# Dispatch transfers of the last layer: one per four experts in place of one per expert, and one more step in the routing

## The chip, the cores and the metric

The kernel runs on one core of a Trainium2 chip. The metric is device time in microseconds (us) of one execution of the whole program, the median over runs. The core has five engines with a queue of instructions each: TensorE (PE, with its weight loads as PEld), VectorE (DVE), ScalarE (ACT), GpSimd (POOL) and SyncE (SP, which here only issues DMAs). An engine runs its own queue in order and waits on semaphores for the others.

## The reference

Four layers follow each other on x of 16 x 256 tokens with 128 features, all in float32; each is `x = x + s(LN(x)) * silu(g(LN(x)))`, with an attention-like part s and a feed-forward part g. The change touches the end of layer 2, whose g is a mixture of 32 experts that is computed for every token and every expert:

```python
sel = jax.nn.sigmoid(x2 @ sel_w)
scores, idx = jax.lax.top_k(sel, K)                                  # K = 4 of 32
gate = (jax.nn.one_hot(idx, E, dtype=sel.dtype) * scores[..., None]).sum(-2)
h = jax.nn.relu(jnp.einsum('bsd,edh->bseh', x2, keys))
moe_out = jnp.einsum('bseh,ehd,bse->bsd', h, values, gate)
```

and layer 3, whose s is a Mamba block in both directions (a scan over time, 256 channels, 16 states) and whose g routes every token to 2 of 16 experts with a limited capacity:

```python
vals, idx = jax.lax.top_k(probs, K)                                  # K = 2 of 16
oh_e = jax.nn.one_hot(idx_flat, E, dtype=x.dtype)
pos = (jnp.cumsum(oh_e, axis=0) * oh_e).sum(axis=1) - 1              # place in the expert's queue
within = (pos < C).astype(x.dtype)                                   # C = 640
expert_inputs = jnp.zeros((E, C, d), x.dtype).at[idx_flat, pos_c].add(x_pair)
expert_outputs = jax.vmap(_mlp)(expert_inputs, w_gate, w_up, w_down)
```

## The kernel before

The 4096 tokens lie in 32 tiles of 128 partitions. Layer 2's experts run in `ffn2`: for each of 8 chunks t of 512 tokens and each of 32 experts e there is one *unit*. PE multiplies by `keys` (L1081, into `f_ph`), ACT takes the relu (L1083, into `f_h`), PE multiplies by `values` (L1112, into `f_po`, two buffers), and DVE adds the product, times the gate, to `f_acc` (L1117, four instructions). A chunk ends with a silu on ACT (L1091) and two DVE operations (L1093, L1095), which give the new x of the chunk.

Between the units a hand-written order advances generators, one step (up to the next `yield`) per unit from e = 4 on: at t = 4 the routing of layer 3 for tiles 0 to 15 (`route.tiles(0, 16, mamba)`), at t = 5 the first work item of Mamba (`mamba.begin()`), at t = 7 the routing of tiles 16 to 27. What a generator has left when the next one begins is run through at once, ahead of expert 4 of that chunk; this happens with the first one at t = 5. The queues of PE, DVE, ACT and POOL hold instructions in just the order in which the program writes them.

`route.tiles` is `norms` (the layer norm of layer 3) and then `places`: logits, softmax, the two best of 16 (L1590 to L1593), a 0/1 mask (L1598 on DVE), the sums of the mask over the tokens ahead and over the tile (two matmuls on PE at L1604), running counts (L1613 to L1619), the place of each token in its expert's queue (L1622 to L1629), and the weights and the int32 index `f_at` (L1632 to L1636). Then four entries per tile go on the list `todo`: two choices j, each with a row of x (i = 0) and its weight and number (i = 1).

`route.scatter` takes one entry off that list and has POOL issue an indirect transfer that writes the 128 rows of a tile to their places in DRAM (`f_xd`, 512 bytes a row, or `f_md`, 8 bytes a row), through `put_rows` (L1358). With `apart` set, as in layer 2, it first puts a memset of one element (L1644) in POOL's queue:

```python
def scatter(self, apart=False):
    if self.todo:
        if apart:
            self.net.nc.gpsimd.memset(self.dot, 0.0)
        i, k, j = self.todo.pop(0)
        rows = self.meta[:, j, k, :] if i else self.net.xn[:, k, :]
        self.net.put_rows((self.xd, self.md)[i], self.at[:, j, k : k + 1], rows, self.sent[i])
```

Before the change layer 2 calls it once per unit with e >= 4. Nothing in POOL's queue waits for the experts: POOL runs a transfer as soon as the instruction before it is done, its index is written, and the transfer eight before it has landed.

What is left on the list goes out in `Mamba3.run`: 16 work items (8 pairs of sequences, two directions), each of 16 units (8 pairs of states times 2 halves of the channels), one transfer after every second unit (L1962), so 128 places in all. A unit of this stage: POOL forms the products (L1827), ACT the factors (L1842), DVE the scans (L1853) and a product with C (L1953), PE spreads C (L1863) and sums over the states (L1957). The products are made two pairs of states ahead. In each work item the first half of the next one (`first`) is run between the units: it stores `m_rows` (L1760) and has POOL do L1782, L1785, L1788 and L1792. The last item also takes the routing of tiles 28 to 31, whose 16 transfers go out at its end; `layer3` issues what is left on the list, and `ffn3` loads `f_md` and `f_xd` for the experts of layer 3.

Of the kernel before, what the change touches and what calls it, by code (L numbers as in the profile page):

```python
# [23 lines left out]
def bc(ap, n):  # L24

    return ap.unsqueeze(len(ap.shape)).to_broadcast([*ap.shape, n])


def bc1(ap, n):

    return ap.unsqueeze(1).to_broadcast([ap.shape[0], n, *ap.shape[1:]])


class Net:
# [988 lines left out]
    def ffn2(self, c, w, left, last):  # L1023
# [35 lines left out]
        route = Route3(self, last)  # L1059
# [12 lines left out]
        with ExitStack() as ctx:  # L1072
            sb = ctx.enter_context(tc.tile_pool(name="l2m", bufs=2))
            ps = ctx.enter_context(tc.tile_pool(name="l2m_ps", bufs=2, space=PSUM))
            long = {4: route.tiles(0, 16, mamba), 5: mamba.begin(), 7: route.tiles(16, 12, mamba)}
            short = now = iter(())
            units = [(t, e) for t in range(NCH) for e in range(NE)]

            def hidden(t, e):
                ph = ps.tile([P, 512], F32, name="f2_ph")  # L1080
                nc.tensor.matmul(ph, lhsT=keys[:, e, :], rhs=self.xnT[:, t * 512 : (t + 1) * 512], start=True, stop=True)  # L1081
                hT = sb.tile([P, 512], F32, name="f2_h", bufs=3)
                nc.scalar.activation(hT, ph, AF.Relu)  # L1083
                return hT

            def gated(t):

                k4 = slice(4 * t, 4 * t + 4)
                yield
                g = sb.tile([P, 4, D], F32, name="gate_t")  # L1090
                nc.scalar.activation(g, acc[:, k4, :], AF.Silu)  # L1091
                yield
                nc.vector.tensor_tensor(g, g, self.s[:, k4, :], ALU.mult)  # L1093
                yield
                nc.vector.tensor_tensor(self.x[:, k4, :], self.x[:, k4, :], g, ALU.add)  # L1095

            ahead = hidden(0, 0)
            for u, (t, e) in enumerate(units):
                if e == 4 and t in long:
                    for _ in now:  # L1100
                        pass
                    now = long[t]
                next(short, None)
                if e >= 4:
                    next(now, None)
                    route.scatter(True)
                hT = ahead
                if u + 1 < len(units):
                    ahead = hidden(*units[u + 1])
                po = ps.tile([P, 4, D], F32, name="f2_po")  # L1110
                for k in range(4):
                    nc.tensor.matmul(  # L1112
                        po[:, k, :], lhsT=hT[:, k * P : (k + 1) * P], rhs=values[:, e, :], start=True, stop=True
                    )
                for k in range(4):
                    n = 4 * t + k
                    nc.vector.scalar_tensor_tensor(  # L1117
                        acc[:, n, :], po[:, k, :], gate[:, n, e : e + 1], acc[:, n, :], ALU.mult, ALU.add
                    )
                if e == NE - 1:  # L1120
                    short = gated(t)
            for f in (short, now):
                for _ in f:
                    pass
# [334 lines left out]
class Route3:  # L1459
# [98 lines left out]
    def places(self, k0, n, mamba):  # L1558
        net, nc, NE = self.net, self.net.nc, self.NE
        kn = slice(k0, k0 + n)  # L1560
        (_, _, c), part = self.parts(n, mamba)
        pr, rep, l = part(0, 0, 24), part(0, 384, 24), part(0, 768, NE)
        mask, pos, fits, over = (part(1, 256 * i, NE) for i in range(4))
        wt, hit, m8 = part(2, 0, NE), part(2, 256, NE), part(2, 784, 8)
        run = c[:, 512 : 512 + 16 * (n + 1)].rearrange("p (n w) -> p n w", w=NE)
        den = c[:, 912 : 912 + n]
        ab = c[:, 928 : 928 + 2 * n].rearrange("p (j n) -> p j n", j=2)
        mx = c[:, 992 : 992 + n]
        pl = mamba.bank()[:, : n * NE].rearrange("p (n w) -> p n w", w=NE)
        for k in range(n):  # L1570
            o = (k0 + k) * P
            nc.tensor.matmul(pl[:, k, :], lhsT=net.xnT[:, o : o + P], rhs=self.rw, start=True, stop=True)
        nc.gpsimd.memset(pr[:, :, NE:], -1.0)
        self.count(hit, [[0, n], [int(self.CAP), NE]], 1, 0)
        self.count(over, [[P * NE, n], [1, NE]], self.rows + 1 + k0 * P * NE, NE)
        yield
        nc.vector.tensor_tensor(l, pl, bc1(self.rb, n), ALU.add)
        nc.vector.tensor_reduce(mx, l, AX.X, ALU.max)
        nc.vector.tensor_tensor(l, l, bc(mx, NE), ALU.subtract)
        yield  # L1580
        nc.scalar.activation(l, l, AF.Exp)
        yield
        nc.vector.tensor_reduce(mx, l, AX.X, ALU.add)
        nc.vector.reciprocal(mx, mx)
        nc.vector.tensor_tensor(pr[:, :, 0:NE], l, bc(mx, NE), ALU.mult)
        yield

        for g in range(0, n, 4):
            for k in range(g, g + 4):
                nc.vector.max(out=m8[:, k, :], in_=pr[:, k, :])  # L1590
            nc.vector.memset(m8[:, g : g + 4, 2:8], -1.0)
            for k in range(g, g + 4):
                nc.vector.match_replace(  # L1593
                    out=rep[:, k, :], in_to_replace=m8[:, k, :], in_values=pr[:, k, :], imm_value=-2.0
                )
            if g + 4 < n:
                yield
        nc.vector.tensor_tensor(mask, pr[:, :, 0:NE], rep[:, :, 0:NE], ALU.not_equal)  # L1598
        yield

        t = mamba.bank()
        pin, tot = (t[:, 256 * j : 256 * j + n * NE].rearrange("p (n w) -> p n w", w=NE) for j in range(2))
        for q, m in ((pin, self.tri), (tot, net.ones)):
            nc.tensor.matmul(q, lhsT=m, rhs=mask, start=True, stop=True)  # L1604
        yield

        nc.vector.tensor_tensor(den, m8[:, :, 0], m8[:, :, 1], ALU.add)
        nc.vector.tensor_scalar_add(den, den, 1e-9)
        nc.vector.reciprocal(den, den)
        nc.vector.tensor_tensor(wt, mask, bc(den, NE), ALU.mult)  # L1610
        nc.vector.tensor_tensor(wt, wt, pr[:, :, 0:NE], ALU.mult)
        yield
        nc.vector.tensor_copy(run[:, 0, :], self.before)  # L1613
        for k in range(n):
            nc.vector.tensor_tensor(run[:, k + 1, :], run[:, k, :], tot[:, k, :], ALU.add)
        nc.vector.tensor_copy(self.before, run[:, n, :])
        nc.vector.tensor_tensor(pos, pin, run[:, 0:n, :], ALU.add)
        nc.vector.tensor_single_scalar(fits, pos, self.CAP, ALU.is_lt)
        nc.vector.tensor_tensor(wt, wt, fits, ALU.mult)  # L1619
        yield  # L1620

        nc.vector.tensor_tensor(pos, pos, hit, ALU.add)  # L1622
        nc.vector.tensor_tensor(pos, pos, over, ALU.subtract)
        nc.vector.tensor_tensor(pos, pos, fits, ALU.mult)
        nc.vector.tensor_tensor(pos, pos, over, ALU.add)
        nc.vector.tensor_tensor(pos, pos, mask, ALU.mult)
        nc.vector.tensor_reduce(ab[:, 0, :], pos, AX.X, ALU.max)
        nc.vector.tensor_reduce(ab[:, 1, :], pos, AX.X, ALU.add)
        nc.vector.tensor_tensor(ab[:, 1, :], ab[:, 1, :], ab[:, 0, :], ALU.subtract)  # L1629
        yield  # L1630
        for j in range(2):
            nc.vector.tensor_tensor(hit, pos, bc(ab[:, j, :], NE), ALU.is_equal)  # L1632
            nc.vector.tensor_tensor(hit, hit, wt, ALU.mult)
            nc.vector.tensor_reduce(self.meta[:, j, kn, 1], hit, AX.X, ALU.add)
        nc.vector.tensor_scalar_add(ab, ab, -1.0)
        nc.vector.tensor_copy(self.at[:, :, kn], ab)  # L1636
        self.todo += [(i, k, j) for k in range(k0, k0 + n) for j in range(2) for i in range(2)]
        yield
# [414 lines left out]
```

## Time and profile before

| | us |
|---|---|
| median of 3 runs | 4148.38 |
| lowest and highest run | 4143.59, 4153.01 |
| the profiled execution | 4153.89 |
| its span, first to last instruction | 4152.2 |
| busy in that span: PE, DVE, ACT, POOL | 3626.3, 2987.9, 2126.9, 1918.5 |
| mean granted clock of TensorE | 0.95 |

The parts that matter here, by the timeline of the same execution: the units of layer 2's experts run up to about 2922, Mamba from there to 3933, the experts of layer 3 to 4152. An instruction's row gives its start, its length, its engine and line, and, in brackets, how long the engine sat idle before it and what ended that wait. Consecutive instructions of one kind are merged into a row (x8). The end of a matmul is modelled. "Granted clock" is the share of its full clock that TensorE got in a stretch. In the chain of waits, "another core or an unknown queue" is a wait whose end the profile can put down to no engine of this core.

### The profile page before, as it was taken

The numbers are of one execution on the slowest core, as the hardware profiler recorded it, in microseconds if no ns is written. First come the engines' busy times: TensorE is split into PE (matmuls) and PEld (weight loads), VectorE is DVE, ScalarE is ACT, GpSimd is POOL, SyncE is SP. The second block draws the span as 40 slices with busy tenths as digits, with TensorE's granted clock in tenths as the row PEclk, the third lists the DMA queues.
The fourth block names the chain that finished last, engine by engine and source line by source line (L and its number), as shares of the span: only waits on it lengthen the run. The fifth ranks groups of instructions, "written<-read, shape, count | busy, mean of one in ns | idle before, by whom it ended". The sixth has DMA issues, their size and how long they took to land. (4 is left out here: it accounts for less than half of the span.)

```text
span 4152.2 us, 61413 instructions
## 1 busy us (share of the span) xinstructions
PE 3626.3 (87%) x21623; PEld 2323.1 (56%) x21623; DVE 2987.9 (72%) x6273; ACT 2126.9 (51%) x4623; POOL 1918.5 (46%) x1979
## 2 busy tenths in 40 slices
PE   5689999875999999999999999769788899899795
PEld 3467777543566666777777776546333333333353
DVE  5467767575888887666666667636888999999834
ACT  2356666642777775444545333223565665666322
POOL 5974444000444443433333100250789877777634
PEclk8899999986999999999999899979899999999998
DMA  8365554320000001000000300010111211121123
GB/s 301 126 212 182 195 194 175 42 78 6 1 1 1 1 1 42 1 1 1 1 1 1 115 1 1 7 35 1 65 66 66 84 64 66 75 82 62 52 81 100
DMA packets 87366, 268.90 MB, mean 65 GB/s; under 512 B 18176, under 2 KB 34088, under 8 KB 81555
## 3 DMA queue, kind: packets, MB, share of 16 engines
q1 hardware_dynamic: 80403, 255.46, 18.0%
q0 software_dynamic: 6656, 9.52, 0.7%
q8 instruction: 172, 2.82, 0.3%
q14 instruction: 135, 1.11, 0.1%
HBM read 192.96 MB, written 71.97 MB: 64 GB/s over the span
## 5 line engine op out<-in xcount | busy, mean ns | idle before, releaser
L1827 POOL TENSOR_TENSOR m_h<-m_B,m_dtu 128x1024 f32<-128x1024 f32 x256 | 597.5, 2358 | 108.2 <-PE m_y L1957 104.1
L1853 DVE TENSOR_TENSOR_SCAN m_h<-m_a,m_h 128x512 f32<-128x512 f32 x512 | 601.3, 1208 | 40.1 <-ACT m_a L1842 34.8
L1957 PE MATMUL m_y<-m_h,ident 128*128 128x512 f32 x1024 | 513.8, 631 | 24.0 <-DVE m_h L1953 23.5
L883 POOL TENSOR_TENSOR a_e<-a_e,a_sm 128x512 f32<-128x512 f32 x256 | 263.8, 1041 | 445.2 <-DVE a_sm L882 351.5
L1117 DVE SCALAR_TENSOR_TENSOR f_acc<-f_po,f_gate,f_acc 128x128 f32<-128x128 f32 x1024 | 287.6, 344 | 219.8 <-PE f_po L1112 152.3
L1112 PEld LDWEIGHTS f_po<-values_sb,f_h 128*128 128x128 f32 x2048 | 277.5, 198 | 207.9 <-issue 130.5
L1957 PEld LDWEIGHTS m_y<-m_h,ident 128*128 128x128 f32 x1024 | 184.1, 195 | 340.3 <-issue 246.1
L398 DVE TENSOR_TENSOR a_e<-a_s,a_c 128x384 f32<-128x384 f32 x256 | 216.3, 845 | 189.9 <-PE a_s L395 183.6
L1189 POOL TENSOR_TENSOR r_g<-r_t 128x256 f32<-128x256 f32 x256 | 183.5, 728 | 360.3 <-DVE r_t L1188 357.2
L1083 ACT ACTIVATE f_h<-f_ph 128x512 f32<-128x512 f32 x256 | 152.2, 596 | 384.4 <-PE f_ph L1081 310.9
L1112 PE MATMUL f_po<-values_sb,f_h 128*128 128x128 f32 x2048 | 282.3, 283 | 71.5 <-ACT f_h L1083 46.6
L1220 ACT ACTIVATE r_e<-r_s,r_mx 128x256 f32<-128x256 f32 x512 | 208.0, 474 | 260.9 <-DVE r_mx L1214 260.8
L1953 DVE TENSOR_TENSOR m_h<-m_h,m_C 128x1024 f32<-128x1024 f32 x256 | 307.1, 1200 | 26.0 <-PE m_C L1863 26.0
L1188 DVE TENSOR_TENSOR r_t<-r_pp,trig_sb 128x512 f32<-128x512 f32 x256 | 169.5, 683 | 207.5 <-PE r_pp L1179 206.3
L876 ACT ACTIVATE a_e<-a_e,a_mx 128x256 f32<-128x256 f32 x512 | 255.1, 500 | 54.6 <-DVE a_sm L882 48.2
L1081 PE MATMUL f_ph<-xnT_sb,keys_sb 128*128 128x512 f32 x512 | 273.6, 618 | 0.4 <-ACT f_gate L1048 0.4
L403 ACT ACTIVATE a_e<-a_e,a_mx 128x128 f32<-128x128 f32 (+1 forms) x512 | 218.6, 453 | 93.0 <-DVE a_mx L399 65.0
L1208 PE MATMUL r_s<-pe_sb,r_g 128*128 128x256 f32 x1024 | 260.7, 388 | 0.0
L373 POOL COPY a_st<-a_p 128x192 f32<-128x192 f32 x256 | 135.7, 532 | 243.5 <-PE a_s L394 160.9
L1842 ACT ACTIVATE m_a<-m_dt,bA_sb 128x510 f32<-128x510 f32 x256 | 170.9, 686 | 141.3 <-DVE m_h L1853 140.4
L1863 PE MATMUL m_C<-m_dbc,ident 32*128 32x512 f32 x512 | 149.1, 655 | 96.6 <-DVE m_h L1953 92.3
L1842 ACT ACTIVATE m_a<-m_dt,fA_sb 128x510 f32<-128x510 f32 x256 | 169.9, 685 | 101.3 <-DVE m_h L1853 100.4
(476 smaller groups left out, 8227.5 us busy)
## 6 DMA issues: line engine op xcount, KB each, us to landing
m_B<-m_rows SPq DMA_DIRECT2D x32, 2048.0 KB
a_p<-pc SPq DMA_DIRECT2D x32, 768.0 KB
a_c<-cs SPq DMA_DIRECT2D x32, 768.0 KB
cs<-a_es SPq DMA_DIRECT2D x64, 256.0 KB
pc<-a_es SPq DMA_DIRECT2D x64, 256.0 KB
a_p<-pc SPq DMA_DIRECT2D x32, 512.0 KB
a_c<-cs SPq DMA_DIRECT2D x32, 512.0 KB
cs<-bg SPq DMA_DIRECT2D x8, 768.0 KB
```

The costliest lines, as they stand in the source:

```text
L403: nc.scalar.activation(e[:, cols], e[:, cols], AF.Exp, bias=mx[:, i : i + 1])
L876: nc.scalar.activation(e[:, i, :], e[:, i, :], AF.Exp, bias=mx[:, i : i + 1], accum_out=sm[:, i : i + 1])
L883: nc.gpsimd.tensor_tensor(e, e, bc(sm, S), ALU.mult)
L1081: nc.tensor.matmul(ph, lhsT=keys[:, e, :], rhs=self.xnT[:, t * 512 : (t + 1) * 512], start=True, stop=True)
L1112: nc.tensor.matmul(po[:, k, :], lhsT=hT[:, k * P : (k + 1) * P], rhs=values[:, e, :], start=True, stop=True)
L1117: nc.vector.scalar_tensor_tensor(acc[:, n, :], po[:, k, :], gate[:, n, e : e + 1], acc[:, n, :], ALU.mult, ALU.add)
L1208: nc.tensor.matmul(s[h][:, i, :], lhsT=G[:, i * P : (i + 1) * P], rhs=w["pe"], start=False, stop=i == 1)
L1827: nc.gpsimd.tensor_tensor(h, st["B"][n // 8][:, m : m + 2, :], bc1(st["dtu"][:, k, :], 2), ALU.mult)
L1842: nc.scalar.activation(f[:, :, 1:], sts[d]["dt"][:, k, :].rearrange("p (b t) -> p b t", b=2)[:, :, 1:], AF.Exp, scale=w[work[d][1]]["A"][: ...
L1853: nc.vector.tensor_tensor_scan(h[:, j, :], ready.pop(0), h[:, j, :], 0.0, op0=ALU.mult, op1=ALU.add)
L1953: nc.vector.tensor_tensor(h, h, sts[d]["C"], ALU.mult)
L1957: nc.tensor.matmul(sts[d]["y"][k], lhsT=net.ident, rhs=h[:, j, :], start=False, stop=n + j == N - 1)
```

## The change

Two edits. In `ffn2` the transfer is issued only at every fourth expert (e = 4, 8, ..., 28) in place of at each one from 4 on. In `places` a `yield` is put between the mask and the two matmuls that sum it, so that these come one step later in all three calls of the routing. Nothing in `Mamba3.run` is edited; its transfers, one per two units, take what is on the list.

```diff
@@ -1103,7 +1103,8 @@
                 next(short, None)
                 if e >= 4:
                     next(now, None)
-                    route.scatter(True)
+                    if e % 4 == 0:
+                        route.scatter(True)
                 hT = ahead
                 if u + 1 < len(units):
                     ahead = hidden(*units[u + 1])
@@ -1600,6 +1601,7 @@
 
         t = mamba.bank()
         pin, tot = (t[:, 256 * j : 256 * j + n * NE].rearrange("p (n w) -> p n w", w=NE) for j in range(2))
+        yield
         for q, m in ((pin, self.tri), (tot, net.ones)):
             nc.tensor.matmul(q, lhsT=m, rhs=mask, start=True, stop=True)
         yield
```

## The prediction

> **What bounds the kernel now.** I read the granted clock and span first (one core, 4152.2 us, mean clock 0.95), then the 40 slices: PE is over 90% busy in most of them and drops to 7 and 6 tenths in the 26th and 27th, where layer 2's experts run. There I took busy time by stretch, the chain of waits, and the timeline of PE and of POOL.
>
> Busy time by stretch (length, then busy us per engine, granted clock, DMA share, GB/s):
>
> ```profile
> core 0: us, PE busy (x) PEld busy (x) DVE busy (x) ACT busy (x) POOL busy (x), PEclk, DMA share, GB/s
> 2500.00:2600.00 100.00, 97.36 (x554) 69.73 (x553) 72.73 (x271) 35.17 (x59) 2.21 (x3) 1.00 0.00 1
> 2660.00:2690.00 30.00, 16.78 (x57) 9.56 (x56) 9.14 (x29) 2.37 (x4) 21.07 (x39) 0.82 0.07 22
> 2690.00:2730.00 40.00, 36.19 (x172) 24.20 (x173) 19.02 (x67) 19.86 (x30) 2.73 (x3) 0.92 0.14 54
> 2745.00:2796.00 51.00, 12.86 (x49) 7.60 (x47) 5.80 (x19) 2.74 (x5) 37.85 (x73) 0.59 0.09 25
> 2796.00:2860.00 64.00, 61.25 (x330) 43.99 (x330) 43.92 (x166) 21.48 (x37) 0.00 (x0) 0.95 0.00 1
> ```
>
> The expert loop is bound by PE, except in two stretches in which PE, DVE and ACT all stand still and only POOL works. POOL's timeline says at what: `DMA_INDIRECT` of L1358, back to back at one per 1.27 us, 20 of them from 2662.8 to 2688.1 and 40 from 2740.4 to 2795.3. Between and after these bursts PE is full again. The chain of waits in the second (start, us, what):
>
> ```profile
> 2747.68 0.60 ACT f_h L1083
> 2748.28 9.94 another core or an unknown queue
> 2758.30 0.60 ACT f_h L1083
> 2758.90 19.68 another core or an unknown queue
> 2778.66 0.60 ACT f_h L1083
> 2779.26 16.20 another core or an unknown queue
> 2795.54 0.61 ACT f_h L1083
> ```
>
> ACT's relu (L1083) waits for nothing but PE's matmul and its own earlier work, yet it starts 7 to 16 us after PE's matmul is over in the record (2750.84 to 2758.30, 2762.73 to 2778.66); something holds back PE's completion as others see it. The first burst, in PE's timeline:
>
> ```profile
> 2678.94 1.05 PE L1112 MATMUL f_po<-values_sb,f_h 128*128 128x128 f32 x8
> 2679.83 1.02 PE L1081 MATMUL f_ph<-xnT_sb,keys_sb 128*128 128x512 f32 x2
> 2692.06 2.08 PE L1112 MATMUL f_po<-values_sb,f_h 128*128 128x128 f32 x8 [11.21 <-DVE f_acc L1117]
> ```
>
> Last, the Mamba stage, by stretches of one work item each (from one `m_rows` store to the next); the first two carry eight transfers each, the last two one and none:
>
> ```profile
> 3152.99:3216.75 63.76, 55.93 (x129) 20.55 (x129) 56.28 (x52) 38.16 (x51) 54.91 (x29) 0.95 0.19 71
> 3216.75:3279.19 62.44, 56.87 (x166) 23.78 (x166) 58.43 (x55) 38.15 (x51) 54.82 (x29) 1.00 0.19 73
> 3279.19:3338.85 59.66, 53.17 (x130) 19.49 (x130) 56.10 (x52) 38.16 (x51) 48.27 (x22) 1.00 0.18 71
> 3338.85:3401.15 62.30, 56.87 (x165) 23.76 (x166) 58.34 (x55) 38.16 (x51) 46.67 (x21) 1.00 0.17 68
> ```
>
> DVE bounds it; POOL is next, and eight transfers cost an odd item 4.1 us and an even one 0.1.
>
> **Part 1, fewer transfers in layer 2.** How many move: 112 transfers are due before the last four tiles. Before, 68 are issued in layer 2 and 44 in Mamba, one per two units. After, POOL's queue holds 21 in layer 2 (each with its 1x1 memset of 0.09 us) and 91 in Mamba, so 47 move past the whole expert loop into slots 44 to 90 of Mamba's 128. The 16 of the last four tiles stay at the end. SP's queue keeps its order.
>
> What the stalls cost. A unit (one expert, 512 tokens) takes 56.05/32 = 1.75 us: the silus of L1091, one per 32 units, lie at 2463.03, 2519.09 and 2575.14. In the first burst the starts of L1112 run 2678.94, 2692.06, 2695.64, 2697.79, the latter ones slow by the clock that fell: (13.12 + 3.58 + 2.15) less 3 x 1.75 = 13.6 us. In the second, four units take 2746.39 to 2796.19, 49.8 less 7.0 = 42.8, and the two after them (2799.76, 2802.74) 3.05 more: 45.8. The silus bear it out: 2741.89 to 2843.78 is 101.9, 45.9 above 56.05. Together **59.4 us on the path**.
>
> What of it stays. The test in the loop does not pace POOL, which waits for no expert: it runs its queue as far as data allow. So the 21 come as 5 at once, 1 between the products of L1782 and L1785, 10 at once behind L1792, then 2 and 3. When does a burst hurt? In the first, signals are on time up to the matmuls of 2672.00 and 10 us late from those of 2673.75, when the ninth transfer had been issued (2673.18); in the second, 1 us late for the matmul of 2745.53 and 5 for that of 2748.85, 8 us into the dense part. It ends with the burst: 3.4 us after its last issue is over (2688.05 to 2691.41), 0.2 us after it in the second. So 5 are free, and 10 (12.7 us) reach the onset at their end: at most 4.7 us over it, plus 3.4 of drain, plus 2.2 of fallen clock (1.83 + 0.40) = 10; at least 0. I take **5**, the middle, since both ends are equally near.
>
> What they cost in Mamba. Slots 44 to 90 are six items, three of each kind: 3 x (63.74 - 59.66) + 3 x (62.45 - 62.30) = **12.7 us**. Ends: 0 if they hide, as in even items; 47 x 1.18 (1.01 and the 0.17 before it) = 55 if POOL set the pace throughout. The stretches above have just this load, so I keep 12.7. Queued behind each transfer on POOL are the products of L1827, for which DVE's scans wait; they are made two steps ahead, which is the cover.
>
> A rule that speaks against this move: the Trainium skill, SBUF — State Buffer, in the section SBUF: two separate sides, warns that descriptor generation on GpSimd is locked out while VectorE holds the shared port, and gives about 620 ns growing to about 3100. Were it so here, an estimate from that page, 1.01 x 5 less 1.01, times 47, adds 190 us of POOL. The trace disagrees for these operations: beside DVE at over 90% the 43 transfers between 2945 and 3281 took 1.007 to 1.011 us, so this gets no chance of its own.
>
> **Part 2, one step more.** `places` yields between the mask (L1598) and the sums on PE (L1604), so these go one unit later in PE's order. Before, PE waits there, 2.8 us at 2636.72 and 2.2 at 2897.73 (5.0 in L1604's waits), and DVE idles 2.0 and 3.5 us behind it. DVE is nearly full in this part, so the gain is bounded by its idle time too: about 2 + 2 = **4 us**. Against it, `tiles(0, 16)` now has three steps left, not two, when they are flushed ahead of expert 4 of t = 5: L1613 to L1619 (4.7 us of DVE) join the 6.2 us of L1622 to L1636. Before, the two lumps cost PE 5.1 us (L1112 at 2643.78, 2649.15, 2652.40: 5.37 + 3.25 - 3.5) and 5.6 (3.86 waiting, 1.74 of fallen clock); one lump of 10.9 costs 3.86 + 4.7 + some 2, the same. Ends: a gain of 8 and a loss of 4. In the last work item the step shifts the index by about a half unit; the 16 transfers behind it end at 3926.8 and are read by the load of 3934.46, so 2 or 3 us are hidden.
>
> **Sum:** -59.4 + 5 + 12.7 - 4 = -45.7 us. The profiled execution took 4153.9 us, 5.5 above the median 4148.4 and just over the highest run, 4153.0; I apply the difference to the median: **4103 us**.
>
> **Rivals.**
> (B) Any run of transfers stalls PE, not only one past eight. For it: the stalls coincide with bursts as a whole. Against it: the first 11 us of the first burst are clean. Then 15 transfers (5 + 10) at 1.27 and two tails of 3.4 + 2.2 stay: 30 in place of 5, 4128 us.
> (C) Slower: the transfers don't cause the stalls, only keep them company, and Mamba's price is paid for nothing: -4 + 12.7 = +8.7, 4157 us. For it: the DMA engines are 7 to 9% busy in the stalls; at the end of Mamba 13 transfers go back to back from 3910.6 to 3926.8 and DVE's scans keep their pace; ACT's wait is put down to no known queue. Against it: two onsets and two ends that fit the bursts within a few us. It decides from the point where PE still loses over 50 us in t = 5 and 6.
> The same page of the Trainium skill (SBUF — State Buffer, section Who interferes with whom) says that a DMA never contends with a compute engine, which by itself would give C; the two stretches above, PE at 12.86 of 51 us beside POOL's 37.85, speak against reading it that way here.
> (D) POOL becomes Mamba's bound: 55 in place of 12.7, 4145 us, no change. Against it: even items pay 0.1.
>
> **How the numbers follow.** Forecast 0.70 (4089 to 4120 by its ends: 0 to 10 of residue, 8 to 17 in Mamba, -8 to +4 of the step, and some 3 us between runs), B 0.16, C 0.09, D 0.05. The range **4086 to 4132** holds the forecast and about two thirds of B. No change means within 0.2%, some 8 us, about what the measurement can tell: faster 0.86 (forecast and B), same 0.06 (D and the near edge of C), slower 0.08.
>
> **What would show it.** Right: the silu spacing of t = 6 within 5 us of 56, no stretch after 2660 with PE below half and the three long waits on "another core or an unknown queue" gone from the chain; 21 memsets of L1646; a residue of a few us just after the ten transfers; Mamba's items at 63.7 and 62.4 up to the eleventh. Wrong: PE empty beside the group of 5 (B), stalls of 10 us and more without a burst (C), items above 64 us (D).

## The result and the profile after

The changed kernel takes 4104.03 us (median of 4, 4099.29 to 4118.51); the kernel before, on the same chip, 4150.69 (4 runs, 4143.59 to 4157.38). The ratio is 0.9891, 95% interval 0.9872 to 0.9911. The profiled execution took 4101.38 us, its span 4099.7.

The two profiled spans differ by 52.5 us, but 6.7 of that is there when the first silu of layer 2 starts (2401.69 us after, 2408.39 before), ahead of all that is edited. So I read from there: 1743.8 us before to the end of the span, 1698.0 after, **-45.8 us**. Busy time by stretch, after (length, then busy us of PE, its weight loads, DVE, ACT and POOL, granted clock, DMA share, GB/s):

```profile
core 0: us, PE busy (x) PEld busy (x) DVE busy (x) ACT busy (x) POOL busy (x), PEclk, DMA share, GB/s
2500.00:2600.00 100.00, 97.37 (x554) 69.72 (x554) 73.58 (x275) 35.74 (x61) 5.07 (x8) 1.00 0.00 1
2657.00:2665.00 8.00, 6.62 (x23) 3.25 (x22) 4.48 (x14) 0.60 (x1) 5.38 (x9) 1.00 0.10 27
2715.00:2735.00 20.00, 14.71 (x82) 10.25 (x83) 9.74 (x35) 5.22 (x10) 12.90 (x21) 1.00 0.06 17
2735.00:2795.00 60.00, 59.60 (x341) 43.01 (x340) 41.74 (x154) 20.82 (x35) 0.00 (x0) 1.00 0.00 1
```

Five transfers leave PE working (second row; of its 1.38 us without work, 1.30 are a wait at 2660.55 that e1 below has too, and without a stall). The ten between 2717.40 and 2730.03 cost it 5.3 of 20 us (third). Then PE is full at full clock (fourth), where before it did 12.86 us of 51 beside the run of 40. The rows of PE with idle time, and the chain of waits, at the end of the ten:

```profile
2728.75 1.13 PE L1113 MATMUL f_po<-values_sb,f_h 128*128 128x128 f32 x8 [2.88 <-issue]
2733.05 1.13 PE L1113 MATMUL f_po<-values_sb,f_h 128*128 128x128 f32 x8 [2.31 <-ACT f_h L1083]
```

```profile
2725.00 0.86 PE f_ph L1081 x2
2725.86 2.88 issue
2728.75 1.13 PE f_po L1113 x8
2729.88 2.01 PE f_ph L1081 x2
2731.89 0.08 ACT f_h L1083
2731.97 0.40 issue
```

The three long waits on "another core or an unknown queue" are gone from the chain. What is left is two gaps; the units' starts (L1113 at 2723.95, 2728.75, 2733.05) give 4.80 + 4.30 less 2 x 1.75 = 5.6 us.

The silus of L1091 lie at 2568.44, 2640.81, 2721.20, 2782.93 and 2858.49: spacings of 72.37, 80.39, 61.73 and 75.56 us for t = 4 to 7, against 73.90, 92.85, 101.89 and 77.64 before. In Mamba, the stretches from one `m_rows` store to the next, with eight transfers each and, in the last row, one:

```profile
3467.40:3531.26 63.86, 56.05 (x130) 20.57 (x130) 56.27 (x52) 38.15 (x51) 54.84 (x29) 0.95 0.19 71
3531.26:3593.68 62.42, 56.87 (x166) 23.77 (x166) 58.42 (x55) 38.15 (x51) 54.78 (x29) 1.00 0.19 73
3593.68:3653.32 59.64, 53.16 (x129) 19.47 (x129) 56.08 (x52) 38.15 (x51) 47.22 (x21) 1.00 0.18 71
```

The items with eight transfers reach six stretches further, and those six grow by 4.17, 0.12, 4.21, 0.12, 4.21 and 0.12 us, 12.95 together.

### The profile page after: what moved, and what is told of

It is laid out like the page before. It is cut to its first block, busy times and chain, and to the rows that moved or that the text cites. A ratio compares the mean times of both kernels' runs of the same rounds, so it can differ in the third digit from the quotient of the medians.

```text
span 4099.7 us, 61363 instructions
## 1 busy us (share of the span) xinstructions
PE 3617.1 (88%) x21623; PEld 2311.1 (56%) x21623; DVE 2983.6 (73%) x6273; ACT 2125.9 (52%) x4623; POOL 1914.6 (47%) x1932
## 5 line engine op out<-in xcount | busy, mean ns | idle before, releaser
L1829 POOL TENSOR_TENSOR m_h<-m_B,m_dtu 128x1024 f32<-128x1024 f32 x256 | 597.6, 2358 | 111.2 <-PE m_y L1959 62.0
L1113 PEld LDWEIGHTS f_po<-values_sb,f_h 128*128 128x128 f32 x2048 | 273.0, 195 | 158.9 <-issue 133.0
L1955 DVE TENSOR_TENSOR m_h<-m_h,m_C 128x1024 f32<-128x1024 f32 x256 | 306.6, 1198 | 28.4 <-PE m_C L1865 28.4
L1113 PE MATMUL f_po<-values_sb,f_h 128*128 128x128 f32 x2048 | 276.8, 279 | 26.3 <-ACT f_h L1083 13.4
L1865 PE MATMUL m_C<-m_dbc,ident 32*128 32x512 f32 x512 | 152.7, 670 | 99.0 <-DVE m_h L1955 91.2
```

The lines of the kernel that those rows point to most:

```text
L1113: nc.tensor.matmul(po[:, k, :], lhsT=hT[:, k * P : (k + 1) * P], rhs=values[:, e, :], start=True, stop=True)
L1829: nc.gpsimd.tensor_tensor(h, st["B"][n // 8][:, m : m + 2, :], bc1(st["dtu"][:, k, :], 2), ALU.mult)
L1955: nc.vector.tensor_tensor(h, h, sts[d]["C"], ALU.mult)
```

## The experiments

The runs were made in groups, each on one chip with the kernel before beside it. The chips have numbers; that of the first comparison is not recorded. The last columns give, for the profiled execution, the time from the first silu to the end of the span (the late part), and the silu spacings at t = 4 to 7. The first silu itself comes anywhere from 2400.45 to 2419.68 us, ahead of all edits, so I judge by these columns; several whole times (e6, a2, k1) lie above the ranges expected for them.

| run | chip | us | before us | ratio, 95% | from first silu | t=4, 5, 6, 7 |
|---|---|---|---|---|---|---|
| before | first | 4150.69 | | | 1743.8 | 73.90, 92.85, 101.89, 77.64 |
| after | first | 4104.03 | 4150.69 | 0.9891 (0.9872 to 0.9911) | 1698.0 | 72.37, 80.39, 61.73, 75.56 |
| e1 | 4 | 4081.50 | 4095.01 | single run | 1678.3 | 69.04, 80.39, 56.05, 73.93 |
| e2 | 4 | 4108.63 | 4095.01 | single run | 1702.2 | 79.82, 80.06, 56.05, 76.10 |
| e3 | 4 | 4080.77 | 4095.01 | single run | 1678.7 | 75.54, 79.14, 56.06, 74.04 |
| e6 | 4 | 4098.69 | 4095.01 | single run | 1677.3 | 69.04, 84.10, 56.05, 72.74 |
| a2 = after | 7 | 4115.41 | 4149.73 | 0.9915 (0.9892 to 0.9937) | 1698.0 | 72.38, 80.39, 61.73, 75.60 |
| k1 | 7 | 4111.93 | 4149.73 | 0.9904 (0.9877 to 0.9931) | 1693.1 | 77.21, 94.56, 56.05, 74.62 |
| e10 | 5 | 4075.79 | 4143.28 | 0.9833 (0.9814 to 0.9852) | 1670.0 | 69.05, 84.10, 56.05, 72.51 |
| e6 again | 5 | 4086.69 | 4143.28 | 0.9855 (0.9832 to 0.9877) | 1683.8 | 72.37, 84.11, 56.06, 72.51 |
| k3 | 5 | 4148.33 | 4143.28 | single run | 1739.0 | 73.91, 92.98, 101.19, 76.90 |
| e8 | 5 | 4092.12 | 4143.28 | single run | 1685.2 | 69.06, 80.40, 56.05, 73.96 |
| e12 | 4 | 4074.24 | 4086.68 | 0.9968 (0.9956 to 0.9980) | 1666.5 | 69.06, 80.35, 56.05, 72.50 |
| a3 = after | 4 | 4105.95 | 4086.68 | 1.0041 (1.0022 to 1.0060) | 1686.9 | 69.06, 80.39, 56.05, 72.29 |

### Each part of the change alone (e1, e2), and the memsets (e3)

e1 has only the step, e2 only the fewer transfers:

```diff
--- before
+++ e1
@@ places
+        yield
         for q, m in ((pin, self.tri), (tot, net.ones)):
--- before
+++ e2
@@ ffn2
-                    route.scatter(True)
+                    if e % 4 == 0:
+                        route.scatter(True)
```

> The extra step alone; the transfers are those of the kernel before (20, then 3, then 40 in layer 2). Theory T1 (a dense run of indirect transfers holds back what PE reports to the other engines): the stalls stay, so the spacing of the silus is within 4 us of before's 92.85 at t=5 less 0 to 5 us for the step, and 98 to 104 at t=6 (before 101.89); time 4145 to 4155. Rival (the step moved the stall out of the way, the transfers did little): t=6 near after's 61.7, time near 4104.

> The thinner transfers alone, without the extra step. T1: t=6 near after's 61.7 us (60 to 64), t=5 at after's 80.4 plus the 4 us that the step was put at (82 to 86), Mamba's items as after's; time about 4107 (4102 to 4112). Rival (the step did it): t=6 near 102, time about 4150.

e3 drops the memset that runs ahead of each transfer:

```diff
@@ ffn2
-                    route.scatter(True)
+                    route.scatter()
```

> The kernel before without the one-element memset that GpSimd runs ahead of each transfer of layer 2. T1 (the transfers themselves): the bursts stay, at about 1.0 to 1.2 us a transfer, and so do the stalls: t=5 88 to 97 us, t=6 92 to 106, time 4140 to 4160. Rival M (the memsets' dense signals hold PE's back): t=6 58 to 64, t=5 near 80, time about 4100.

What came fitted neither side. e1 has all its transfers of before, in the same runs of 20 and 40 and 1.27 us apart, and no stall: t=6 took 56.05 us. And the kernel before, on this chip 4, took 4095.01 us, not 4150. A stretch of e1 in which POOL issues nothing but its run of 40 (the columns are those of the table of stretches above, here and below):

```profile
2718.00:2768.00 50.00, 50.00 (x285) 36.14 (x285) 33.63 (x118) 17.04 (x30) 40.75 (x77) 1.00 0.10 28
```

PE is busy for all 50 us. So e3 says nothing on the memsets here, for there was no stall to remove, and e2's fewer transfers had nothing to gain: it has the longest late part of the four, 1702.2 us, of which some 5.9 are dips of the granted clock at t=4 (its 79.82 against 73.90 before).

### Is it the chip? (a2, a3)

> The changed kernel once more, against the kernel before on the same chip. On the chip of the runs e1 to e6 the kernel before took 4095 us (it took 4151 on the chip of the first comparison), and e1, with all its transfers in the same runs of 20 and 40, had no stall. Theory T2 (the stall belongs to a state of the chip or of the place that the program gets there, and the change only gains where it is present): where the kernel before takes about 4150, after takes about 4104 and the silu spacing at t=6 is 57 to 63; where the kernel before takes about 4095, after takes about 4090 to 4101 (the step's gain of some 5 to 10 less Mamba's 11.6) and the spacing at t=6 is 56. Rival (4095 was a chance execution): the kernel before takes 4143 to 4157 and after 4099 to 4118 on any chip.

On chip 7 the kernel before took 4149.73 us and the changed one 0.9915 of it; its late part is again 1698.0 us and t=6 61.73, as on the first chip. A later group of runs was on chip 4 again:

> The changed kernel, once more on whichever chip this is, from the first silu to the end 1698 us where the kernel before stalls (before 4137 to 4159 us, ratio about 0.989 to 0.992, t=6 61.7). Theory T2, where the kernel before takes about 4095 (no stall): t=6 56.05, 1692 from the first silu on, and a ratio between 0.998 and 1.004: layer 2 gains the step's 5 us and Mamba loses 11.6.

There the change **loses**: 1.0041, 1.0022 to 1.0060. Its ten transfers, again 1.27 us apart, cost PE nothing; the work item of Mamba with eight transfers costs what it did:

```profile
2720.00:2735.00 15.00, 15.00 (x86) 10.70 (x85) 11.15 (x38) 5.32 (x10) 11.71 (x21) 1.00 0.07 23
...
3087.10:3150.90 63.80, 55.99 (x129) 20.57 (x128) 56.25 (x52) 38.13 (x52) 54.81 (x29) 0.95 0.19 71
```

Theory T2 fits, with 1.0041 just outside its range and the late part, 1686.9, 5 us below the 1692: chips 7 and 5 stall, and that of the first comparison, which may be one of them; chip 4 doesn't, in two groups of runs, though four of its profiles have dense transfers (e1, e2, e3, a3). Whether it is the chip itself or something that the program was given on it, the runs don't tell apart. The kernel before has no profile there; e3, which is that kernel but for the memsets, has a late part of 1678.7 us and a3 one of 1686.9, 8.2 more: up to the last silu a3 is 7.1 shorter, from there on, where Mamba is, 15.3 longer. The medians of a3 and the kernel before differ by 19.3; the profiled execution of a3 was itself 8.6 us below its median, and where the rest lies no profile shows.

### What in the transfers stalls PE (k1, k3, e8)

k1 makes two tests in one run: the first 19 transfers without memsets, the others tied to each expert's relu output, so that POOL can't run ahead:

```diff
@@ ffn2
-                    route.scatter(True)
+                    route.scatter(ahead)
@@ Route3.scatter
-            if apart:
-                self.net.nc.gpsimd.memset(self.dot, 0.0)
+            if apart is not None and len(self.sent[0]) >= 10:
+                a = apart[:1, 0:1]
+                self.net.nc.gpsimd.tensor_tensor(self.dot, a, a, ALU.subtract)
```

> The kernel before with two edits in one run: the first 20 transfers of layer 2 have no memset ahead of them (still about 1.27 us apart), the rest are tied to each expert's relu output by a subtraction of one element from itself, so that they come one per 1.75 us in place of one per 1.27. Where the kernel before shows its stalls (4150 us): T1 (dense transfers do it, memsets don't) expects the first stall to stay (silu spacing at t=5 88 to 97) and the second to go (t=6 56 to 62), time about 4100 to 4108. Rival M (the memsets do it): t=5 near 80, t=6 near 56. Rival N (number alone): t=5 near 93, t=6 85 to 102. Where the kernel before shows no stall (4095 us): t=5 79 to 84 and t=6 56 under every theory.

It ran on a chip that stalls. First the stretch of the 19 dense transfers, then that of the paced ones; below them, ACT's row out of the first:

```profile
2673.00:2701.00 28.00, 17.07 (x57) 9.74 (x58) 7.45 (x26) 2.60 (x5) 18.48 (x19) 0.74 0.08 24
2758.00:2808.00 50.00, 50.00 (x288) 36.42 (x287) 32.84 (x117) 17.22 (x29) 33.22 (x56) 1.00 0.07 20
```

```profile
2700.17 0.60 ACT L1083 ACTIVATE f_h<-f_ph 128x512 f32<-128x512 f32 x1 [15.10 <-remote]
```

Without a single memset the first stall stays (t=5 94.56): the relu waits 15.10 us for "remote", which is no engine of this core, and starts 3 us after the last of the 19 is over (2697.13). At one transfer per 1.75 us, 28 in a row cost PE nothing (t=6 56.05). So the memsets are out, and so is the number alone: the pace does it, or that POOL waits for the units between two transfers; k1 doesn't tell these two apart.

What is late, as far as the records show, is PE's signal. In the trace of the kernel before, the update of PE's semaphore that lets the relu of 2758.30 go is recorded at 2758.22; the matmul that it waits for is over at 2750.84 by its modelled end.

k3 sends the 32 small rows (8 bytes each) of the first call ahead of its large ones (512 bytes):

```diff
@@ places
-        self.todo += [(i, k, j) for k in range(k0, k0 + n) for j in range(2) for i in range(2)]
+        new = [(i, k, j) for k in range(k0, k0 + n) for j in range(2) for i in range(2)]
+        self.todo += new if k0 else sorted(new, key=lambda x: -x[0])
```

> The kernel before with the first call's transfers in another order: all 32 of the small rows (8 bytes each) first, then the 512-byte rows. So the first run of 20 holds small rows only, and the run of 40 nine small and 31 large ones. Where the kernel before stalls: T1 (each transfer counts the same, whatever its bytes): the spacings of the silus stay, t=4 and t=5 together 162 to 172 us and t=6 96 to 106. Rival L (the bytes: 64 KB a transfer): t=4 and t=5 together about 153 to 158 and t=6 75 to 95. Rival S (rows of 8 bytes): the first two together 170 or more, t=6 56 to 64. Where it doesn't stall: about 155 and 56.

t=4 and t=5 took 166.89 us together (before 166.75), t=6 101.19 (101.89). The first stall, now of small rows alone, and the second, mostly of large ones, are as they were; the bytes don't matter. In the run of 40 PE does 12.40 and then 3.78 of 20 us:

```profile
2741.00:2761.00 20.00, 12.40 (x57) 7.74 (x55) 5.70 (x18) 3.20 (x6) 16.69 (x31) 0.82 0.09 24
2761.00:2781.00 20.00, 3.78 (x10) 2.21 (x10) 1.13 (x4) 0.60 (x1) 16.00 (x31) 0.50 0.14 49
```

e8 is the changed kernel with a plain transfer of 64 KB at each of the other experts:

```diff
@@ ffn2
                         route.scatter(True)
+                    elif route.todo:
+                        nc.gpsimd.memset(route.dot, 0.0)
+                        o = len(route.plain) * P
+                        rows = self.xn[:, len(route.plain) % 16, :]
+                        route.plain.append(nc.gpsimd.dma_start(route.aside[o : o + P, :], rows))
@@ Route3.__init__
+        self.aside = dram.tile([64 * P, D], F32, name="f3_aside")
+        self.plain = []
```

> The changed kernel, with a plain (not indirect) transfer of 64 KB by GpSimd, to rows that nothing reads, at each of the other experts: the same places and the same memset ahead of each as the kernel before, but only every fourth transfer is indirect. The output is the reference's. Where the kernel before stalls: T1 in its wide form (any dense run of GpSimd's transfers) expects the stalls back, t=4 and t=5 together 160 to 172 us and t=6 90 to 105. Rival I (only indirect ones do it): t=6 56 to 63, t=4 and t=5 together about 153. Where it doesn't stall: about 153 and 56.

POOL's rows, and the stretches from 2718 on:

```profile
2719.23 1.02 POOL L1364 DMA_INDIRECT f_xd<-xn_sb,f_at  x1 [0.23 <-issue]
2720.25 0.09 POOL L1109 MEMSET m_x<- 1x1 f32 x1
2720.28 0.55 POOL L1112 DMA_DIRECT2D f_aside<-xn_sb  x1
```

```profile
2718.00:2738.00 20.00, 20.00 (x114) 14.43 (x114) 14.07 (x48) 7.09 (x13) 18.40 (x53) 1.00 0.23 74
2738.00:2758.00 20.00, 20.00 (x117) 14.57 (x116) 13.03 (x47) 6.87 (x12) 10.05 (x29) 1.00 0.13 44
```

A row of 40 transfers without a gap, POOL 92% busy in the first stretch, memsets denser than ever (one per 0.57 us between two indirect transfers), three times the bytes per second, and PE never waits: t=6 is 56.05. (t=4 and t=5 are 149.5 together, below the 153 expected, for t=4 has no dip of the clock here.) Ten of the 40 are indirect, every fourth, 3.04 us apart; ten at 1.27 cost 5.6 us in the changed kernel, on the first chip and on chip 7. POOL waits for no unit in e8, so for these ten the pace alone is enough. In the expert loop, then, it is indirect transfers back to back, on the chips that have it; not POOL's load, not the bytes, not the semaphores of memsets.

A dense run is not enough by itself, though. At the end of Mamba every profile has 13 indirect transfers 1.27 us apart, without memsets, from 3910.61 to 3926.81 in that of the kernel before. DVE there starts a pair of scans per 3.36 us throughout, and its first L1883, which waits for PE, starts 5.54 us after the last scan does; in e3, on chip 4, it starts 5.58 after. So these 13 cost nothing on the first chip, nor on chips 5 and 7 (5.59 in k3, 5.58 in a2, by the same measure), where ten cost 5.6 us in the expert loop. What the loop adds to the transfers (its signals follow each other faster, one unit per 1.75 us) no run separates.

### Pacing in place of thinning (e6, e10, e12)

If the pace is what counts, no transfer needs to move to Mamba. e6 has the step, and ties every transfer of layer 2 to the relu:

```diff
@@ ffn2
-                    route.scatter(True)
+                    route.scatter(ahead)
@@ Route3.scatter
-            if apart:
-                self.net.nc.gpsimd.memset(self.dot, 0.0)
+            if apart is not None:
+                self.net.nc.gpsimd.tensor_tensor(self.dot, apart[:1, 0:1], apart[:1, 0:1], ALU.subtract)
```

> The extra step, a transfer at every expert as before, but the one-element memset ahead of each is replaced by a subtraction of one element of that expert's relu output from itself, so that GpSimd can't run ahead of the experts: one transfer per 1.75 us in place of one per 1.27 us, all 63 in layer 2. T1 by rate (the queue fills when transfers are issued faster than they finish; they take about 1 us each): no stall, t=6 57 to 62 us, Mamba's items as before's (two of a pair 59.65 and 62.3 from the sixth on), time 4104 - 11.6 - 5 = about 4087 (4082 to 4096). Rival N by number (any run of more than some ten transfers stalls, whatever its pace): t=6 85 to 102, time 4130 to 4150.

> The kernel of e6 on this chip: paced transfers and the extra step. T1 by rate: from the first silu to the end 1675 to 1680 us whether or not the kernel before stalls on this chip (1677.3 on the chip without stalls); against a before at 4150 a ratio of about 0.984. Rival N: 1695 to 1745 where the kernel before takes about 4150.

On chip 4 e6 took 4098.69 us, above the 4082 to 4096 expected, its first silu being the latest of all (2419.68); with no stall there it decided nothing. On chip 5, which stalls, t=6 is 56.06: the pace suffices. The late part was 1683.8, above the 1675 to 1680 expected: t=4 3.3 us and four work items of Mamba together 6.9 longer than in the first run, 3.3 back at the end. e10 adds that Mamba issues transfers in every other work item alone:

```diff
@@ Mamba3.run
-                if k:
+                if k and (d % 2 == 0 or d + 1 == len(work)):
                     route.scatter()
```

> The paced transfers and the extra step as in e6, and in Mamba the transfers only in every other work item, in those whose pair of spacings they lengthen by 0.12 us and not by 4.2. Read from the first silu to the end of the span, e6 took 1677.3 us, the kernel before 1743.8, after 1698.0. T1 by rate and a price of 4.2 us for each of the other items: two of those that e6 has are spared, so 1677.3 - 8.4 = 1669 (1664 to 1674) on any chip. Rival (the price of those items goes over to the others): 1677. Rival N (number alone stalls where the chip stalls): over 1700.

1670.0 us, in the range. The odd items carry none now, and each takes 59.65 or 59.66:

```profile
3086.25:3145.90 59.65, 53.16 (x129) 19.48 (x129) 56.10 (x52) 38.15 (x51) 49.13 (x24) 1.00 0.18 72
```

The price of pacing is t=5, 84.10 against 80.39. ACT's rows in e10:

```profile
2717.38 0.60 ACT L1083 ACTIVATE f_h<-f_ph 128x512 f32<-128x512 f32 x1 [2.16 <-POOL m_x L1645]
2721.06 0.60 ACT L1083 ACTIVATE f_h<-f_ph 128x512 f32<-128x512 f32 x1 [0.71 <-POOL m_x L1645]
2724.73 0.60 ACT L1083 ACTIVATE f_h<-f_ph 128x512 f32<-128x512 f32 x1 [3.08 <-POOL m_x L1645]
```

The relu waits for a buffer that POOL has yet to read, behind steps of 2.36 us. e12 gives it six:

```diff
@@ ffn2
-                hT = sb.tile([P, 512], F32, name="f2_h", bufs=3)
+                hT = sb.tile([P, 512], F32, name="f2_h", bufs=6)
```

> The kernel of e10 with six buffers in place of three for the experts' relu output, which GpSimd now reads one element of ahead of each transfer. In e10 three relus in the sixth row of units wait for that read while GpSimd works through four long steps of Mamba's (2.36 us each), and the matmuls behind them 1.66 to 1.70 us each: t=5 took 84.1 us there, 80.4 in e1. Theory: with three more buffers the wait goes, t=5 80.4 (80 to 81.5), from the first silu to the end 1670.0 - 3.7 = 1666 (1662 to 1671, a dip of the granted clock of 3.3 us in t=4 in or out). Rival (the transfers' lag is caught up a little later, by the same time): t=5 near 84 or t=6 above 58, the sum unchanged at 1670.

t=5 is 80.35, the late part 1666.5. e10 is 0.9833 of before on chip 5, which stalls; the given change has 0.9891 on the first chip and 0.9915 on chip 7. e12 is 0.9968 on chip 4, which doesn't, where the change has 1.0041. e12 wasn't run on a chip that stalls.

## Why the prediction was right

| step | predicted | measured |
|---|---|---|
| first stall | -13.6 | -13.7: t=5 92.85 before, 79.14 in e3, both without the step |
| second stall, less what stays | -45.8 + 5 | -40.2: t=6 101.89 to 61.73 |
| the step, first call of the routing | -2 | -3.6: t=4 73.90 to 69.05, t=5 79.14 to 80.39 |
| the step, second call | -2 | -2.1: t=7 77.64 to 75.56 |
| Mamba | +12.7 | +11.5: six items 12.95, two earlier ones -1.4 |
| not foreseen | | +3.3 at t=4, -1.1 elsewhere |
| sum | -45.7 | -45.8 |

**The stalls.** The price was right, and so was the rule of the onset in this loop: 5 transfers free, 10 costing 5.7 (t=6 61.73 against 56.05). That it came so near the 5 is chance, since 5 was the middle of 0 to 10. Rival B, all dense transfers, is refuted by the five: PE has no stall beside them. What the prediction left out is that the stall isn't the kernel's alone. Rival C (the transfers only keep the stalls company, Mamba's price is for nothing) was given 0.09. On chips 5 and 7 k1, e8 and e10 refute it; on chip 4, where there is no stall, its balance comes out all the same, a loss. The profile of before could not show that, being from one chip. One point that C had for it, the 13 transfers at the end of Mamba, stands: they cost nothing on any chip, and the onset is a rule of the expert loop, not of every dense run. The sentence of the Trainium skill set beside it there, SBUF — State Buffer, in the section Who interferes with whom, that a DMA never contends with a compute engine, agrees with chip 4 (PE 50.00 of 50.00 us beside dense indirect transfers) and with the plain transfers on chip 5. The indirect ones on chips 5 and 7 do make PE's signals late; whether that is contention as the page means it, no run shows.

**The step.** The wait at the sums (L1604, now L1606) falls from 5.0 us to 1.0 in the two calls, as put. First before, then after:

```profile
2636.72 0.67 PE L1604 MATMUL m_pp<-m_l,f_tri 128*128 128x256 f32 x2 [2.83 <-DVE m_l L1598]
2897.73 0.86 PE L1604 MATMUL m_pp<-m_l,f_tri 128*128 128x192 f32 x2 [2.22 <-DVE m_l L1598]
```

```profile
2633.34 0.67 PE L1606 MATMUL m_pp<-m_l,f_tri 128*128 128x256 f32 x2 [0.56 <-DVE m_l L1599]
2650.15 1.09 PE L1708 MATMUL m_pp<-ident,s_sb 128*128 128x128 f32 x4 [5.20 <-DVE m_l L1619]
2836.86 0.56 PE L1606 MATMUL m_pp<-m_l,f_tri 128*128 128x192 f32 x2 [0.46 <-DVE m_l L1599]
```

The joined lump costs PE a longer wait, 5.20 us, than either of the two had (3.46 and 3.69). The prediction counted 2 us of gain for each of these calls: the first gave 3.6, the second 2.1. The 4.85 us at t=4 come twice: 73.90 to 69.05 (e10) without a dip of the clock, and 77.21 (k1) to 72.38 (a2) on one chip, both with the same dip. The 79.14 of e3 is from chip 4, without memsets, and both the price of the first stall and the step's cost at t=5 rest on it; by e2, also without the step, at 80.06, they would be 12.8 and 0.3. The sum of the two rows stays the same.

**Mamba.** The size was right, the working too simple. I said that POOL is next to the bound and that its two-step lead covers it. In the odd items it doesn't: DVE's scans wait 1.24 us for POOL's products (L1829), PE idles, its granted clock falls, and then DVE waits for PE. Stretches of 8 us within one item of 63.80, after, and two of DVE's rows in them:

```profile
3120.00:3128.00 8.00, 5.20 (x10) 1.75 (x9) 7.33 (x7) 2.76 (x4) 7.80 (x5) 0.73 0.00 0
3128.00:3136.00 8.00, 8.00 (x17) 3.47 (x16) 5.98 (x7) 1.38 (x2) 7.62 (x6) 0.84 0.02 8
3136.00:3144.00 8.00, 8.00 (x21) 3.14 (x20) 6.05 (x6) 2.20 (x4) 7.81 (x4) 1.00 0.03 8
```

```profile
3120.67 2.34 DVE L1855 TENSOR_TENSOR_SCAN m_h<-m_a,m_h 128x512 f32<-128x512 f32 x2 [1.24 <-POOL m_h L1829]
3130.09 0.69 DVE L1885 TENSOR_TENSOR m_yg<-m_y,m_uz 128x512 f32<-128x512 f32 x1 [2.02 <-PE m_y L1959]
```

At 7.80 of 8 us POOL is full and PE at 0.73 of its clock. Neither of the two waits is there in the item of 59.64; with 0.7 more at L1955 <- L1865 they make up 4.0 of the 4.16 us. That the first wait brings on the others is read from their order. An odd item comes out at 62.43 (clock 0.97) or 63.8 (0.95) with the same eight transfers; without any, 59.65.

**The dip.** The 3.3 us at t=4 are no work of the change: PE is busy throughout and has the clock taken from it.

```profile
2609.00:2624.00 15.00, 15.00 (x79) 11.56 (x78) 7.02 (x24) 4.05 (x7) 0.00 (x0) 0.77 0.00 0
```

The first profile of before had no such dip, a2 and k1 had it, a3 and e1 not; in e2 and e3, without the step, t=4 is 5.9 and 1.6 us above the 73.90 of before. The dip cost the first pair of profiles 3.3 us of what the change gains; the step gave 1.7 more than put, Mamba cost 1.2 less, and 1.1 came from elsewhere. That the sum came within 0.1 us is luck of that size.

## What to carry to other kernels

Where engines stand still beside a dense run of GpSimd's indirect transfers and the profile names no engine of this core that they wait for, try to tie each transfer to a unit of the work rather than send fewer: here all of them then fit, at one per 1.75 us, and nothing has to move into a stage where it costs something. The operation that ties reads a buffer, which needs spares. And a gain that rests on a stall whose releaser the profile can't name is to be measured on several chips before it is believed: here the same edit is 0.9891 on one and 1.0041 on another.

## What the runs showed of the hardware

- The same 40 indirect transfers, 1.27 us apart, cost PE 45.8 us on the first chip and nothing on chip 4. The one other difference found is in the records: a transfer that has landed updates its semaphore 16 times on chip 4, and of the 3328 updates of the program's 208 indirect transfers the profiles of chip 4 hold 3310 to 3328, those of the other chips 1769 to 2368 (without e8, which has more transfers), with a stall or without. So only the profiles of chip 4 give a time to landing. Why is open.

```profile
DMA to landing us min/median/max: 2.1/2.6/6.5
```

  That is e1's, for the lines of L1358.
- On chips that stall, indirect transfers of 1 KB (128 rows of 8 bytes) hold PE's signals back in the expert loop as long as those of 64 KB (k3), and plain ones of 64 KB at twice the rate not at all (e8). At the end of Mamba 13 indirect ones in a row delay nothing.
- The granted clock fell to 0.77 over 15 us of unbroken PE work in some executions of the same program and in others not, at a cost of 3.3 us.
